# A graph convolution on one core: the preparation in front of the edge loop is cut to the first 512 tiles, and the rest is spread over the first pass

## The chip, the core and the metric

The kernel runs on one core of a Trainium2 chip. The metric is the device time of one execution in microseconds (us). TensorE is called PE, VectorE DVE, ScalarE ACT, GpSimd POOL and SyncE SP; DMAs are issued from the queues of SP, ACT and POOL (SPq, ACTq, POOLq in the profile) and run on 16 DMA engines that all queues share.

## The reference

There are N = 12500 nodes with 128 features and E = 400000 edges with 20 attributes and a weight each. The targets `dst` are sorted.

```python
h = jnp.maximum(_layernorm(x, axis=-1), 0.0)
h = h @ W_in2f.T                                     # N x 128
Wij = smu(edge_attr @ W_f1.T + b_f1) @ W_f2.T + b_f2   # E x 128, smu is a smooth GELU-like bend
Wij = Wij * edge_weight[:, None]
x_ij = h[dst] * Wij                                  # gather by dst, which is sorted
agg = segment_sum(x_ij, src, num_segments=N)         # scatter by src, which is random
out = x + smu(agg @ W_o1.T + b_o1) @ W_o2.T + b_o2
```

So for each edge a row of `h` is read at the edge's target, multiplied by a filter that two small layers compute from the attributes, and summed into the row of its source.

## The kernel before

**Tiles.** 128 edges are a tile; there are NT = 3125 tiles. Four tiles are a group (NG = 782), eight tiles a "super" (391), and the supers are split into seven passes (`PARTS`, six of 59 supers = 118 groups, and a last one of 37). Nodes are in NB = 98 bins of 128.

**Gather.** Since `dst` is sorted, the targets of a super lie within a window of 128 rows of `h`. `load(s)` on SP brings the attributes of super s (`f`), its targets relative to the first one (`rbc`, from the DRAM tensor `rel_dram`), reads the first target from `base_i` into a register and loads 128 rows of `h` from there (`hw`, from the DRAM tensor `h_dram`; three bf16 parts of each row). `pick` makes a one-hot matrix of `rbc` on DVE, and `gather` multiplies by it on PE. `hide`, `bend`, `smooth` and `weigh` are the two layers of the filter, `take` and `mix` the product, `turn` four PE transposes.

**Scatter.** `send` scales the rows by the edge weights on ACT and issues four indirect DMAs per group on POOL (line 562), one for each tile: each edge's row goes to a slot in the part of `buf<k>` (DRAM) that belongs to its source's bin. `bins`, `count`, `read` and `number` compute the slots from `hi_b` (the source's bin) with PE and DVE. While pass k+1 runs, `parts` reads back the slots of pass k (`fetch`), and sums each bin by a one-hot matmul (`choose`, `add`) into `agg`. After the last pass, the last slots are summed and the output layers run.

**Order.** PE, DVE, ACT and SP run in the order in which the code is written (`tc.manual_schedule`). In loop iteration g the engines turn and send group g, mix group g+1, hide and count group g+2 and make bins of group g+3, so DVE, ACT and PE run ahead of POOL by as much as the six buffers `ms` allow. An engine works strictly in order: what stands behind a waiting instruction waits too. This holds for the queues of SP and ACT as well, in which the DMA issues stand among the other instructions. A further wait is set by the framework: DMAs from SP and ACT share eight completion counters in turn, and a DMA waits until the DMA eight issues before it, on the same counter, has landed.

**In front of the loop (lines 216 to 313).** All of `dst` and `src` is loaded (ACT's queue, lines 221 and 228), all of `w_sb`, the first HEAD = 8 bins of x on SP (line 223), and the rest of x in four DMAs on POOL (lines 226 and 227). x is held in the memory of `agg` (`x_sb`). Then the relative targets of all tiles are computed (`rel`: a PE broadcast of the first targets, line 256; a DVE subtraction, line 259), transposed on PE (line 266), cast on ACT (line 267) and written to `rel_dram` on SP (line 268); their limits are reduced (lines 276 and 277); `hi_b` and `lo_b` are cut from `src` (lines 289 to 293); the statistics of the layer norm (`stats`), and the rows of `h` (`rows_of_h`, six steps for four bins: `normed` on DVE, `turned` on PE, `cut` on ACT, `product` on PE, `first_part` and `other_parts` on ACT and DVE, then a DMA into `h_dram`) are made for the first eight bins; two weights and a bias are folded.

**In the first pass.** `others` yields the remaining steps, and `step()` is called three times in each group: first the statistics of the 90 other bins, two at a time followed by two empty steps (141 calls, 47 groups), then one for the deviations, then six for each four bins of `h` (138 calls, 46 groups). The first pass reads only rows of `h` below HEAD * 128 (`base_i` is held to that by line 284, and `bad` records if it didn't suffice; a slow fallback at the end, which is not entered here, serves that case).

**Clearing.** Before slots are scattered into `buf<k>`, their tail is cleared from a zero tile on SP: 48 DMAs of 387 KB for the first pass within its first 38 groups, while the scatter already runs, and those of pass k+1 during pass k.

Of the kernel before, what the change touches and what calls it, by code (L numbers as in the profile page):

```python
# [9 lines left out]
F32 = mybir.dt.float32  # L10
BF = mybir.dt.bfloat16
I32 = mybir.dt.int32
F16 = mybir.dt.float16
AF = mybir.ActivationFunctionType
ALU = mybir.AluOpType
# [24 lines left out]
def gnn_kernel(  # L40
# [85 lines left out]
    nc.vector.memset(onesb, 1.0)  # L126
    bad = const.tile([P, 4 + 2 * EPOCHS], F32, name="bad")
    nc.vector.memset(bad, 0.0)
# [39 lines left out]
    HEAD = 8  # L168
# [47 lines left out]
    with tc.tile_pool(name="prep", bufs=1) as prep, \  # L216
            tc.tile_pool(name="node", bufs=3) as node, \
            tc.tile_pool(name="nps", bufs=2, space=PSUM) as nps:
        dst_i = prep.tile([P, NT], I32, name="dst_i")
        src_i = prep.tile([P, NT], I32, name="src_i")  # L220
        nc.scalar.dma_start(dst_i, dst_col)
        nc.vector.memset(x_sb[:, NB - 1, :], 0.0)
        nc.sync.dma_start(x_sb[:, 0:HEAD, :], bin_rows(x, 0, HEAD))
        nc.sync.dma_start(w_in, w_in_t)
        for a, n in chunks(NB - 1 - HEAD, 30):
            nc.gpsimd.dma_start(x_sb[:, HEAD + a:HEAD + a + n, :], bin_rows(x, HEAD + a, n))
        nc.gpsimd.dma_start(x_sb[:LASTB, NB - 1, :], x[(NB - 1) * P:N, :])
        nc.scalar.dma_start(src_i, src_col)
        nc.scalar.dma_start(w_sb, w_col)
        nc.vector.memset(w_f1, 0.0)  # L230
        nc.scalar.dma_start(w_f1[0:R, :], w_f1_t)
        nc.scalar.dma_start(w_f1[R:R + 1, :], b_f1)
        nc.scalar.dma_start(w_f2, w_f2_t)
        nc.scalar.dma_start(w_o1, w_o1_t)
        nc.scalar.dma_start(w_o2, w_o2_t)
        nc.scalar.dma_start(b1, b_o1.rearrange("o p -> p o"))
        nc.scalar.dma_start(b2row, b_f2)
        nc.scalar.dma_start(b2, b_f2.rearrange("o p -> p o"))
        nc.scalar.dma_start(bo2, b_o2.to_broadcast([P, P]))

        nc.vector.memset(zero, 0.0)
        clear(0, len(cleans) - 1, nc.sync)
        zero_b = prep.tile([P, 3 * D], BF, name="zero_b")
        nc.vector.memset(zero_b, 0.0)
        nc.scalar.dma_start(h_dram[NB * P:N + WIN, :], zero_b[:N + WIN - NB * P, :])


        nc.vector.tensor_copy(base_i[:, :], dst_i[0:1, 0:NT:SUP])
        base_f = prep.tile([1, NS], F32, name="base_f")
        nc.vector.tensor_copy(base_f, base_i)  # L250
        rel = prep.tile([P, NT], F32, name="rel")
        nc.vector.tensor_copy(rel, dst_i)
        S = GRP * P // SUP
        for a, n in chunks(NS, S):
            pb = nps.tile([P, S, SUP], F32, name="pb")
            nc.tensor.matmul(pb[:, :n], ones1, base_f[:, a:a + n].unsqueeze(2).to_broadcast([1, n, SUP]),
                             start=True, stop=True)
            w = min(NT - a * SUP, n * SUP)
            nc.vector.tensor_sub(rel[:, a * SUP:a * SUP + w], rel[:, a * SUP:a * SUP + w],
                                 pb.rearrange("p s t -> p (s t)")[:, :w])  # L260
        for a, m in chunks(NT // P, GRP) + [(NT // P, 0)]:
            pd = nps.tile([P, GRP, P], F32, name="pd")
            rb = node.tile([P, GRP, P], BF, name="rb")
            if m:
                for j in range(m):
                    nc.tensor.transpose(pd[:, j, :], rel[:, (a + j) * P:(a + j + 1) * P], ident)
                nc.scalar.activation(rb[:, :m], pd[:, :m], AF.Copy)
                nc.sync.dma_start(rel_dram[0, a * P * P:(a + m) * P * P].rearrange("(c t e) -> t c e", t=P, e=P),
                                  rb[:, :m])
            elif NT % P:  # L270
                m = NT % P
                nc.tensor.transpose(pd[:m, 0, :], rel[:, a * P:NT], ident)
                nc.scalar.activation(rb[:m, 0], pd[:m, 0], AF.Copy)
                nc.sync.dma_start(rel_dram[0, a * P * P:].rearrange("(t e) -> t e", e=P), rb[:m, 0])
        lh = prep.tile([P, 2], F32, name="lh")
        nc.vector.tensor_reduce(lh[:, 0:1], rel, op=ALU.min, axis=AX.X)
        nc.vector.tensor_reduce(lh[:, 1:2], rel, op=ALU.max, axis=AX.X)
        nc.vector.tensor_scalar(bad[:, 0:1], lh[:, 0:1], 0.0, None, op0=ALU.is_lt)
        nc.vector.tensor_scalar(bad[:, 1:2], lh[:, 1:2], float(WIN - 1), None, op0=ALU.is_gt)
        most = prep.tile([1, 1], F32, name="most")  # L280
        early = eps_of[0][1] + 3
        nc.vector.tensor_reduce(most, base_f[:, :early], op=ALU.max, axis=AX.X)
        nc.vector.tensor_scalar(bad[0:1, 2:3], most, float(HEAD * P - WIN), None, op0=ALU.is_gt)
        nc.vector.tensor_scalar(base_i[:, :early], base_f[:, :early], float(HEAD * P - WIN), None, op0=ALU.min)


        for a, n in chunks(NT, 625):
            part = node.tile([P, 625], I32, name="part")
            nc.vector.tensor_scalar(part[:, :n], src_i[:, a:a + n], 7, None, op0=ALU.arith_shift_right)
            nc.vector.tensor_copy(hi_b[:, a:a + n], part[:, :n])  # L290
            part = node.tile([P, 625], I32, name="part")
            nc.vector.tensor_scalar(part[:, :n], src_i[:, a:a + n], P - 1, None, op0=ALU.bitwise_and)
            nc.vector.tensor_copy(lo_b[:, a:a + n], part[:, :n])


        for b in range(HEAD):
            stats(node, b)
        deviations(0, HEAD)
        for b, n in chunks(HEAD, GRP):
            four = [node.tile([P, GRP, P], F32, name=f"four{i}") for i in range(3)]  # L300
            for step in rows_of_h(b, n, *four, node.tile([P, GRP, 3, D], BF, name="hs"),
                                  lambda name: nps.tile([P, GRP, P], F32, name=name)):
                step()

        nc.vector.tensor_scalar(w_f2, w_f2, GC, None, op0=ALU.mult)
        nc.vector.tensor_scalar(w_o2, w_o2, GC, None, op0=ALU.mult)

        nc.vector.tensor_scalar(bz, b1, ZS, None, op0=ALU.mult)
        b1w = prep.tile([P, P], F32, name="b1w")
        nc.vector.tensor_scalar(b1w, onesb, b1, LIN, op0=ALU.mult, op1=ALU.mult)  # L310
        pb1 = nps.tile([P, GRP, P], F32, name="pd")[:, 0, :]
        nc.tensor.matmul(pb1, b1w, w_o2, start=True, stop=True)
        nc.vector.tensor_add(bo2, bo2, pb1)

# [28 lines left out]
    with tc.tile_pool(name="ld", bufs=4) as ld, \  # L343
# [9 lines left out]
        nc.vector.tensor_copy(irow_ps, irow)  # L353
        NF = 4
        fbufs = []
        for i in range(NF):
            fb = ld.tile([P, SUP * P], F32, name=f"f{i}", bufs=1)
            nc.vector.memset(fb, 1.0)
            fbufs.append(fb)
# [7 lines left out]
        def load(s):  # L367
            if s >= NS:
                return
            t0, nt = sups[s]  # L370
            e0, n = t0 * P, nt * P
            fb = fbufs[s % NF]
            nc.sync.dma_start(fb[0:R, :n], f_t[:, e0:e0 + n])
            rb = ld.tile([P, SUP * P], BF, name="rbc")
            nc.sync.dma_start(rb[:, :n], rel_dram[:, e0:e0 + n].to_broadcast([P, n]))
            hw = ld.tile([P, 3 * D], BF, name="hw")
            at = nc.sync.value_load(base_i[0:1, s:s + 1], min_val=0, max_val=N)
            nc.sync.dma_start(hw, h_dram[bass.ds(at, WIN), :])
            loaded[s] = (fb, rb, hw)
# [255 lines left out]
        for s in range(3):  # L635
            load(s)
        for s in range(2):
            pick(s)
        for g in range(3):
            bins(g)  # L640
        count(0)
        read(0)
        count(1)
        read(1)
        number(0)
# [5 lines left out]
        weigh(0)  # L651
        gather(0)
        take(0)
        mix(0)
        smooth(1)
        cleared = at_first = done = 0
        work = []

        hs = edge.tile([P, GRP, 3, D], BF, name="hs", bufs=1)

        def others():
            for b, n in chunks(NB - HEAD, 2):
                yield lambda b=b, n=n: [stats(edge, HEAD + b + j) for j in range(n)]
                yield None
                yield None
# [8 lines left out]
        def step():  # L674
            f = next(h_steps, None)
            if f:
                f()
# [227 lines left out]
```

## Time and profile before

| | |
|---|---|
| median of 3 runs | 4286.98 us (4285.12 to 4287.03) |
| profiled execution | 4295.33 us, of it span 4293.6 us |
| mean granted PE clock in it | 0.966 |
| busy in the span | PE 87%, DVE 74%, POOL 71%, ACT 66% |
| indirect DMAs on POOL | 3125, mean 967 ns |
| first indirect DMA starts at | 93.53 us |

The profiled execution is 8.35 us longer than the median of the runs. A page's row names a line, an engine, an operation and its tiles, then the count, the busy time and the mean of one in ns, and the idle time of the engine before it with what ended it. In a timeline a row starts with the start and the duration in us, and ends with the idle time before it in brackets.

### The profile page before, as it was taken

The numbers are of one execution on the slowest core, as the hardware profiler recorded it, in microseconds if no ns is written. First come the engines' busy times: TensorE is split into PE (matmuls) and PEld (weight loads), VectorE is DVE, ScalarE is ACT, GpSimd is POOL, SyncE is SP. The second block draws the span as 40 slices with busy tenths as digits, with TensorE's granted clock in tenths as the row PEclk, the third lists the DMA queues.
The fourth block names the chain that finished last, engine by engine and source line by source line (L and its number), as shares of the span: only waits on it lengthen the run. The fifth ranks groups of instructions, "written<-read, shape, count | busy, mean of one in ns | idle before, by whom it ended". The sixth has DMA issues, their size and how long they took to land.

```text
span 4293.6 us, 74022 instructions
## 1 busy us (share of the span) xinstructions
PE 3745.7 (87%) x18332; PEld 2305.2 (54%) x18596; DVE 3177.7 (74%) x8458; ACT 2825.2 (66%) x11054; POOL 3029.8 (71%) x3137
## 2 busy tenths in 40 slices
PE   4877786999997999979999979999889999799977
PEld 2334443655554655545655546555556555466666
DVE  5876675877776877768877768777678777688856
ACT  2777786776766777657766667767667767566610
POOL 1777677777777777777777777777777777777710
PEclk9999998999999999989999999999999999899989
DMA  6955565766665766647666657666576666466666
GB/s 186 218 144 165 162 185 150 204 208 197 196 180 182 211 207 195 202 148 209 208 201 196 197 164 213 195 198 202 146 205 197 188 183 187 145 204 197 192 192 179
DMA packets 457334, 808.89 MB, mean 188 GB/s; under 512 B 82228, under 2 KB 258630, under 8 KB 456512
## 3 DMA queue, kind: packets, MB, share of 16 engines
q1 hardware_dynamic: 328136, 573.65, 47.4%
q0 software_dynamic: 101504, 212.48, 15.5%
q10 hardware_dynamic: 27256, 17.94, 1.4%
q8 instruction: 150, 2.46, 0.3%
q14 instruction: 288, 2.36, 0.2%
HBM read 449.68 MB, written 354.07 MB: 187 GB/s over the span
## 4 chain that ended last, share of the span: by engine, by line
PE 33%; DMA 15%; DVE 13%; ACT 5%; issue 3%; POOL 1%; ACTq 0%; DVEq 0%; POOLq 0%; SPq 0%
DMA buf<-ms,ix 13%; PE pw L529 8%; PE pg L607 8%; PE pu L479 6%; PE ph L510 5%; PE pt L549 4%; DVE se L594 4%; DVE mt L539 2%; DMA hg<-in_x 2%; ACT ms L559 2%; DVE sm L495 1%; ACT ge L487 1%; ACT jk L457 1%; DVE co L414 1%; DVE agg L620 1%
## 5 line engine op out<-in xcount | busy, mean ns | idle before, releaser
L562 POOL DMA_INDIRECT buf<-ms,ix x3125 | 3023.1, 967 | 1065.4 <-issue 278.4
L559 ACT ACTIVATE ms<-pt,w_sb 128x128 f32<-128x128 f32 x3125 | 905.0, 390 | 501.9 <-DMA buf<-ms,ix 287.0
L607 PEld LDWEIGHTS pg<-se,rw 128*128 128x128 f32 x7840 | 1075.3, 193 | 168.2 <-issue 23.4
L607 PE MATMUL pg<-se,rw 128*128 128x128 f32 x7840 | 1098.7, 276 | 19.7 <-DVE se L594 19.7
L457 ACT ACTIVATE jk<-pc,nbig 128x98 f32<-128x98 f32 x3125 | 1029.3, 354 | 12.9 <-PE pc L428 12.5
L529 PE MATMUL pw<-sm,w_f 128*128 128x512 f32 x1564 | 897.5, 656 | 27.1 <-DVE sm L495 19.6
L539 DVE SCALAR_TENSOR_TENSOR mt<-pw,b,hg 128x512 f32<-128x512 f32 x782 | 583.8, 747 | 416.7 <-ACT hg L518 414.2
L479 PE MATMUL pu<-f,w_f 128*128 128x512 f32 x1564 | 808.1, 599 | 2.6 <-DVE sm L495 2.5
L549 PE MATMUL pt<-ident,mt 128*128 128x128 f32 x3125 | 497.6, 282 | 347.3 <-DVE mt L539 343.8
L487 ACT ACTIVATE ge<-pu 128x512 f32<-128x512 f32 x782 | 469.4, 600 | 471.9 <-PE pu L479 459.9
L594 DVE TENSOR_TENSOR se<-irow_ps,rw 128x1536 f32<-128x1536 f32 x327 | 571.8, 1749 | 162.0 <-DMA rw<-buf 135.8
L457 ACT ACTIVATION_READ_ACCUMULATOR jk<-pc,nbig 128x1 f32 x3125 | 682.9, 219 | 0.0
L495 DVE SCALAR_TENSOR_TENSOR sm<-pu,ge 128x512 f32<-128x512 f32 x782 | 536.1, 686 | 186.0 <-ACT ge L487 175.2
L510 PE MATMUL ph<-oh,hw 128*128 128x512 bf16 (+1 forms) x2082 | 635.2, 387 | 15.5 <-issue 2.0
L518 ACT ACTIVATE hg<-ph 128x512 f32<-128x512 f32 x782 | 469.4, 600 | 228.8 <-PE ph L510 226.8
L549 PEld LDWEIGHTS pt<-ident,mt 128*128 128x128 f32 x3125 | 352.5, 142 | 439.3 <-DVE mt L539 434.5
L414 DVE TENSOR_TENSOR co<-co,po 128x98 f16<-128x98 f16 x2351 | 502.3, 214 | 81.2
L510 PEld LDWEIGHTS <-hw 128*128 128x128 bf16 x2346 | 234.2, 100 | 560.6 <-issue 460.0
L400 DVE TENSOR_TENSOR po<-irow_ps,hi_b 128x392 f16<-128x392 f32 x782 | 433.9, 555 | 0.0
L529 PEld LDWEIGHTS pw<-sm,w_f 128*128 128x128 f32 x1564 | 237.7, 191 | 170.7 <-DVE sm L495 167.1
L427 PE MATMUL pc<-co,ones_h 128*128 128x392 f16 x782 | 257.7, 330 | 14.0 <-DVE co L414 14.0
L479 PEld LDWEIGHTS pu<-f,w_f 128*128 128x128 f32 x1564 | 250.4, 194 | 23.6 <-DVE sm L495 4.1
(114 smaller groups left out, 1675.2 us busy)
## 6 DMA issues: line engine op xcount, KB each, us to landing
rw<-buf SPq DMA_DIRECT2D x326, 774.0 KB
buf<-zero SPq DMA_DIRECT2D x294, 387.0 KB
rbc<-rel_dram SPq DMA_DIRECT2D x390, 256.0 KB
buf<-ms,ix POOLq DMA_INDIRECT x3125
hw<-h_dram SPq DMA_DIRECT2D x391, 96.0 KB
f<-in_f_t SPq DMA_DIRECT2D x390, 80.0 KB
buf<-zero SPq DMA_DIRECT2D x49, 258.0 KB
h_dram<-hs SPq DMA_DIRECT2D x24, 384.0 KB
```

Of the source, the lines that this page charges most:

```text
L414: nc.vector.tensor_add(co[:, j], co[:, j - 1], po[:, j - 1])
L457: nc.scalar.activation(jk, pc[:, j], AF.Relu, bias=nbig, accum_out=sl[:, j:j + 1])
L479: nc.tensor.matmul(pu[:, :n], w_f1, loaded[g // PER][0][:, o:o + n], start=True, stop=True)
L495: nc.vector.scalar_tensor_tensor(sm[:, :n], units_of.pop(g)[:, :n], LIN, hidden[g][:, :n], op0=ALU.mult, op1=ALU.add)
L510: nc.tensor.matmul(ph[:, :n], hw[:, q * D:(q + 1) * D], oh[:, o:o + n], start=(q == 0), stop=(q == 2))
L529: nc.tensor.matmul(pw[:, :n], w_f2, hidden.pop(g)[:, :n], start=True, stop=True)
L539: nc.vector.scalar_tensor_tensor(mt[:, :n], pws.pop(g)[:, :n], b2, rows_of.pop(g)[:, :n], op0=ALU.add, op1=ALU.mult)
L549: nc.tensor.transpose(pt[:, j, :], mt[:, j * P:(j + 1) * P], ident)
L559: nc.scalar.activation(ms[:, j, 0:P], pt[:, j], AF.Copy, scale=w_sb[:, t + j:t + j + 1])
L562: i = nc.gpsimd.indirect_dma_start(out=bufs[k][:, :], out_offset=bass.IndirectOffsetOnAxis(ap=ix[:, j:j + 1], axis=0), in_=ms[:, j, :], in ...
L594: nc.vector.tensor_tensor(se[:, :m], irow_ps.unsqueeze(1).to_broadcast([P, m, P]), rows_in[c][:, :m, P:P + 1].to_broadcast([P, m, P]), op= ...
L607: nc.tensor.matmul(pgs[0][:, g, :], rows_in[c][:, o, 0:P], sel[c][:, o, :], start=(q == 0), stop=(q == Q[k] - 1))
```

## The change

The pools and the code in front of the loop go. What the first pass needs of it (the relative targets, bins and places of the first CH = 512 tiles, that is 64 supers, and the rows of `h` of HEAD = 4 bins) is made within the loop's own pools, in an order written out by hand together with the loop's first steps. The same for the other six chunks of 512 tiles becomes nine steps each (`head_of`), one bin's statistics after each; then the other statistics, the deviations, six steps for each four bins of `h`, and the folding of the output bias: COUNT = 276 steps. `step()` spreads them evenly over 318 calls (106 of the 118 groups). The bulk of x moves from POOL's queue to ACT's, in three DMAs of 31 bins and one of 84 rows, behind the small loads; `w_sb` comes in two parts. The check of the limits is reduced at the end.

```diff
-    HEAD = 8
+    HEAD = 4
...
-        nc.scalar.dma_start(dst_i, dst_col)
-        nc.sync.dma_start(x_sb[:, 0:HEAD, :], bin_rows(x, 0, HEAD))
-        for a, n in chunks(NB - 1 - HEAD, 30):
-            nc.gpsimd.dma_start(x_sb[:, HEAD + a:HEAD + a + n, :], bin_rows(x, HEAD + a, n))
-        nc.scalar.dma_start(src_i, src_col)
-        nc.scalar.dma_start(w_sb, w_col)
...
-        nc.vector.tensor_copy(rel, dst_i)
-        for a, n in chunks(NS, S):
...
-        for a, m in chunks(NT // P, GRP) + [(NT // P, 0)]:
...
-        for b in range(HEAD):
-            stats(node, b)
-        deviations(0, HEAD)
-        for b, n in chunks(HEAD, GRP):
...
+        def head_of(c):
+            a, n = c * CH, min(CH, NT - c * CH)
+            s0, m = a // SUP, (n + SUP - 1) // SUP
+            rw = rowp.tile([P, ROWS, ROW], F32, name="rw").rearrange("p q r -> p (q r)")
+            di, si, rel = rw[:, 0:n].bitcast(I32), rw[:, CH:CH + n].bitcast(I32), rw[:, 2 * CH:2 * CH + n]
+            if c:
+                rb = hs[:, :, 0, :]
...
+            def fetched():
+                nc.sync.dma_start(di, dst_col[:, a:a + n])
+                nc.sync.dma_start(si, src_col[:, a:a + n])
+            def based():
+                nc.vector.tensor_copy(base_i[:, s0:s0 + m], di[0:1, 0:n:SUP])
+                nc.vector.tensor_copy(base_f[:, :m], base_i[:, s0:s0 + m])
+                nc.vector.tensor_copy(rel, di)
+            def spread():
...
+                nc.tensor.matmul(flat, ones1, base_f[:, :m].unsqueeze(2).to_broadcast([1, m, SUP]),
+                                 start=True, stop=True)
+            def lowered():
+                nc.vector.tensor_sub(rel, rel, kept[0].rearrange("p j e -> p (j e)")[:, :n])
+            def turned():
...
+                    nc.tensor.transpose(pd[:w, j, :], rel[:, o:o + w], ident)
+            def written():
...
+                    nc.scalar.activation(rb[:, :whole], kept[0][:, :whole], AF.Copy)
+                    nc.sync.dma_start(rel_dram[0, a * P:(a + whole * P) * P].rearrange("(c t e) -> t c e", t=P, e=P),
+                                      rb[:, :whole])
...
+            def limits():
+                nc.vector.tensor_reduce(lh[:, 0, c:c + 1], rel, op=ALU.min, axis=AX.X)
+                nc.vector.tensor_reduce(lh[:, 1, c:c + 1], rel, op=ALU.max, axis=AX.X)
+            def bounded():
...
+            def binned():
+                nc.vector.tensor_scalar(di, si, 7, None, op0=ALU.arith_shift_right)
+                nc.vector.tensor_copy(hi_b[:, a:a + n], di)
+            def placed():
+                nc.vector.tensor_scalar(di, si, P - 1, None, op0=ALU.bitwise_and)
+                nc.vector.tensor_copy(lo_b[:, a:a + n], di)
...
+        one = head_of(0)
+        one["fetched"]()
+        nc.scalar.dma_start(x_sb[:, 0:HEAD, :], bin_rows(x, 0, HEAD))
+        nc.scalar.dma_start(w_in, w_in_t)
...
+        nc.scalar.dma_start(w_sb[:, 0:CH], w_col[:, 0:CH])
+        for i in range(NF):
+            fill(i)
+        nc.vector.memset(zero, 0.0)
+        clear(0, len(cleans) - 1, nc.scalar)
+        nc.vector.memset(x_sb[:, NB - 1, :], 0.0)
+        for a, n in chunks(NB - 1 - HEAD, 31):
+            nc.scalar.dma_start(x_sb[:, HEAD + a:HEAD + a + n, :], bin_rows(x, HEAD + a, n))
+        nc.scalar.dma_start(x_sb[:LASTB, NB - 1, :], x[(NB - 1) * P:N, :])
+        nc.scalar.dma_start(w_sb[:, CH:NT], w_col[:, CH:NT])
+        nc.scalar.dma_start(w_o1, w_o1_t)
+        nc.scalar.dma_start(w_o2, w_o2_t)
+        nc.scalar.dma_start(b1, b_o1.rearrange("o p -> p o"))
+        nc.scalar.dma_start(b2row, b_f2)
+        nc.scalar.dma_start(bo2, b_o2.to_broadcast([P, P]))
...
         for s in range(3):
+            nc.sync.dma_start(fbufs[s][0:R, :], f_t[:, s * SUP * P:(s + 1) * SUP * P])
+        one["based"]()
+        one["spread"]()
+        one["bounded"]()
+        one["lowered"]()
+        one["turned"]()
+        one["written"]()
+        nc.vector.tensor_scalar(w_f2, w_f2, GC, None, op0=ALU.mult)
+        for b in range(HEAD):
+            stats(edge, b)
+        deviations(0, HEAD)
+        rw = rowp.tile([P, ROWS, ROW], F32, name="rw")
+        for step in rows_of_h(0, HEAD, *[rw[:, j * GRP:(j + 1) * GRP, 0:P] for j in range(3)], hs, bank):
+            step()
+        for s in range(3):
             load(s)
-        for s in range(2):
-            pick(s)
-        for g in range(3):
-            bins(g)
-        count(0)
-        read(0)
-        count(1)
-        read(1)
-        number(0)
+        one["binned"]()
+        bins(0)
         hide(0)
         bend(0)
         smooth(0)
         hide(1)
         bend(1)
         weigh(0)
+        count(0)
+        read(0)
+        one["placed"]()
+        pick(0)
         gather(0)
+        number(0)
         take(0)
         mix(0)
         smooth(1)
+        bins(1)
+        count(1)
+        read(1)
+        pick(1)
+        bins(2)
...
         def others():
-            for b, n in chunks(NB - HEAD, 2):
-                yield lambda b=b, n=n: [stats(edge, HEAD + b + j) for j in range(n)]
-                yield None
-                yield None
+            yield one["limits"]
+            yield zeroed
+            left = list(range(HEAD, NB))
+            for c in range(1, NC):
+                it = head_of(c)
+                for name in ("fetched", "based", "spread", "lowered", "turned", "written", "binned", "placed", "limits"):
+                    yield it[name]
+                    if left:
+                        yield lambda b=left.pop(0): stats(edge, b)
+            while left:
+                two, left = left[:2], left[2:]
+                yield lambda two=two: [stats(edge, b) for b in two]
             yield lambda: deviations(HEAD, NB)
...
+            yield output_bias
+
+        COUNT = 2 + 18 * (NC - 1) + (NB - HEAD - 9 * (NC - 1) + 1) // 2 + 1 + 6 * -(-(NB - HEAD) // GRP) + 1
...
         def step():
-            f = next(h_steps, None)
-            if f:
-                f()
+            nonlocal taken_steps, slot
+            slot += 1
+            while taken_steps < COUNT and taken_steps * 3 * (eps_of[0][1] * PER - 12) < slot * COUNT:
+                next(h_steps)()
+                taken_steps += 1
...
+        nc.vector.tensor_reduce(ends[:, 0:1], lh[:, 0], op=ALU.min, axis=AX.X)
+        nc.vector.tensor_reduce(ends[:, 1:2], lh[:, 1], op=ALU.max, axis=AX.X)
+        nc.vector.tensor_scalar(bad[:, 0:1], ends[:, 0:1], 0.0, None, op0=ALU.is_lt)
+        nc.vector.tensor_scalar(bad[:, 1:2], ends[:, 1:2], float(WIN - 1), None, op0=ALU.is_gt)
```

## The prediction

> **What bounds the kernel now.** I read the page first, then POOL's timeline at the start, in the plain part and in the h part of the first pass, then the mixing instruction (line 539, once per group) as a clock of the other engines, then the timeline of the first 100 us with the SP and ACT queues.
>
> ```profile
> PE 3745.7 (87%) x18332; PEld 2305.2 (54%) x18596; DVE 3177.7 (74%) x8458; ACT 2825.2 (66%) x11054; POOL 3029.8 (71%) x3137
> L562 POOL DMA_INDIRECT buf<-ms,ix x3125 | 3023.1, 967 | 1065.4 <-issue 278.4
> ...
> 93.53 1.04 POOL L562 DMA_INDIRECT buf<-ms,ix  x1 [86.25 <-DVE ix L466]
> ...
> 602.11 0.96 POOL L562 DMA_INDIRECT buf<-ms,ix  x1 [0.30 <-ACT ge L487]
> 603.38 0.96 POOL L562 DMA_INDIRECT buf<-ms,ix  x1 [0.30 <-ACT jk L457]
> ...
> 474.95 1.39 POOL L562 DMA_INDIRECT buf<-ms,ix  x1 [2.38 <-ACT hs L208]
> ```
>
> PE is busiest on the page (87%), but POOL sets the pace: two scatters start 1.265 us apart whatever the idle time is put down to (0.96 busy, 0.30 between), so a group of four costs 5.06 us, and 3125 of them 3953 us of the 4293.6. Idle POOL time beyond the 0.30 is in two places: 93.53 us before the first scatter, and an h part around 420 to 575 us.
>
> ```profile
> L539 DVE SCALAR_TENSOR_TENSOR mt<-pw,b,hg x5: 745/746/750, 462.9 to 486.9; 128x512 f32<-128x512 f32 x5
> ...
> L539 DVE SCALAR_TENSOR_TENSOR mt<-pw,b,hg x5: 743/746/751, 123.6 to 139.8; 128x512 f32<-128x512 f32 x5
> ...
> 597.00:645.00 48.00, 36.68 (x38) 1.00 0.70 194
> 440.00:488.00 48.00, 32.34 (x32) 0.93 0.52 155
> ...
> PE pg L193 <- DVE rw L187: 21.1, 12, 1.8
> ```
>
> Four groups of the other engines take 16.2 us beside the statistics (4.05 each), also without any step (597 to 613), but 24.0 us (6.0 each) with three h steps a group. At 4.05 they run ahead of POOL: from mixing a group to its first scatter is 2.3 us at group 0 and saturates at about 26.5 us (six `ms` buffers); when they bound, it is 4.9. The lead of 21.6 us is eaten from group 47 on; from group 64 POOL gets 32 scatters where the plain part gets 38. By its start times in the trace, groups 64 to 89 take 156.7 us instead of 26 x 5.06 = 131.6: 25 us lost. At the end of the pass the engines wait for POOL (DVE sits 20.6 us for the first read-back), so a lead left there is worth nothing.
>
> ```profile
> 8.06 0.36 ACTq L233 DMA_DIRECT2D w_f<-in_w_f_t  x1
> 30.36 0.36 ACTq L234 DMA_DIRECT2D w_o<-in_w_o_t  x1
> 30.36 0.49 DVE L176 BATCH_NORM_STATS2 st<-agg 128x6 f32<-128x128 f32 x2 [27.71 <-DMA agg<-in_x]
> ...
> 70.50 0.50 SPq L375 DMA_DIRECT2D rbc<-rel_dram  x1
> 72.39 0.37 SPq L378 DMA_DIRECT2D hw<-h_dram  x1
> ```
>
> The 93.5 us are 30 of loading, 40 of preparing all tiles, 23 from the first `rbc` to the first scatter. And ACT's queue stood 22 us before line 234: its completion counter was that of x's first eight bins, which landed at 30.36 (the statistics start then too). That matters below.
>
> **The change, part by part.**
>
> *The start.* A first guess is "only 1 MB to load": wrong, because bulk x now stands in ACT's own queue, and the compiled order with its waits shows who waits: ACT's last load (`bo2`) for the second x chunk, the first `rel_dram` write on SP for the third, the first `rbc` load for the rest of `w_sb`. ACT's first activation stands behind `bo2`. So:
> - DVE's memsets: preface 1.3, four small ones about 1.0, four `f` at 1.07, `zero` 0.70: 7.6 us. Then ACT clears the last bin and issues x at about 8; first packets 2 us later, as in the trace (issue 0.75, first packet 2.05).
> - x is 11,988 rows of 512 B. Such packets on ACT's queue take 28 ns in the output stage: / 16 engines, 7 us a chunk. Chunk two lands at about 25, three at 32, the rest of `w_sb` (1.34 MB at the 350 GB/s of the first 20 us) at 36.
> - ACT free at 25.4, table load 1.28, cast 0.60. Then the h chain: table 1.28, `rstd` 0.30, and from the reciprocal to the `h_dram` issue 8.4 in before for eight bins (59.86 to 68.22), I take 7.5 for four: 36.4. `rel_dram` lands about then.
> - `rbc` issued at 36.8, landed 3.4 later (as the first one in before) at 40.2; `hw` issued 3.4 after the last `h_dram` issue (69.0 to 72.39 in before): 39.8, landed 42.
> - DVE behind the h rows: bins and slots 0.8 + 1.5, `smooth` 0.69: 39.5. In before `smooth(0)` to the first scatter is 7.35 us (86.18 to 93.53). The hand-made order puts `count(0)`, `count(1)`, `bins(1)`, and `read(1)` ahead of group 0's transposes and rows: 1.0 + 0.8 on PE, 1.5 on DVE, about 1.3 on ACT: 12 in all.
>
> First scatter at about 52: **-41.5 us**. Ends: 47 (DMA faster, PE out of its slow start, where a 512-column pass took 0.9 us and not 0.5) and 62 (ACT held until all of x and `w_sb` landed).
>
> *The removed preparation* of chunks 1 to 6 (two reductions of 3.4, casts, 24 transposes) is in that difference. It comes back in the pass. Per chunk by DVE rows: 512/3125 of the 3.4 reductions twice 0.6, subtraction 0.69, cast 0.34, base 0.26, four bin instructions at 0.40: 4.1; PE two broadcast passes 1.0 and four transposes 1.1; ACT 0.6; three DMAs on SP. Together 6.8 us of engine time. Four bins of h are 6.6 us (DVE 1.1 + 0.69 + 0.69, PE 1.1 + 1.15, ACT 0.60 + 0.62 + 0.63) and cost 2 x (6.03 - 4.05) = 4.0 us of the engines' common pace. So I take 4.5 per chunk, plus waits: `based` makes DVE wait for `dst` two or three calls after its fetch, 3 to 7 us; a 256 KB load among the clears lands 5 to 7 us after issue (`rbc` in the trace from 100 to 165 us). Queued behind it are `smooth` and `bins`, then PE and ACT. One long and two short waits, 5 us in all, go into the pace; the first chunk comes with no lead, **+2 us**. (SP's later loads are three supers ahead.)
>
> Here a rule speaks against the change. The Trainium skill's "DMA: Bandwidth & Descriptors", section "Anatomy of one DMA", gives about 2.0 us fixed plus bytes/436 GB/s for a transfer: 2.6 us for each 256 KB piece by estimate, 31 us for the twelve, if they were waited for in turn. The trace's busy pass has 5 to 7 us each instead, more than the rule; but waited for is only what the two calls between do not cover. I use the trace.
>
> *Lead.* Chunks: 41 groups at 4.05 + (6 x 4.5 + 5)/41 = 4.83, below 5.06: lead +9, from 2.3 to about 10. Then 20 calls of statistics, 7.7 groups at 4.05: +8, so 18, that is 13 above the bound state's 4.9.
>
> *The h part.* 24 x 6 = 144 steps at 276/318 per call are 55 groups at 4.05 + 2.60 x 0.66 = 5.77: deficit 39 us, less 13 of lead: 26 lost. Before 25: **+1**. (Full lead: 18 lost. No lead: 39. Bound below: if the cover grew with thinner steps, 0.) The last 12 groups rebuild 12 us, more than the boundary needs (about 10).
>
> *Casts beside POOL.* The skill's "SBUF — State Buffer", section "Who interferes with whom", says that copy, cast and tensor_scalar on DVE can take the port pair shared with GpSimd and block it outright. While the cuts ran before the loop, POOL was idle; now 30 stand beside scatters. A full block of 0.4 each would be 12 us. In the trace the 42 scatters that overlap a `normed` instruction last 1.095 us against 0.965, those beside `pick` 0.993 against 0.963. By those rows 30 x 0.03 to 0.13, 1 to 4 us: **+1**.
>
> *The rest.* POOL loses four DMA issues (6.7 us, before its long wait: 0). Four small DVE reductions at the end stand among idle DVE time of 1 to 2 us per step: 0, at worst +0.7. The `h_dram` padding, `w_o2` and `bo2` folds (1.2 us DVE) go into the lead. HEAD 4 holds the early reads below row 384; no cost.
>
> Sum: -41.5 + 2 + 1 + 1 = -37.5. Against the profiled 4295.33 that is 4258; the median of the runs is 8.35 lower, so 4249.
>
> **The rivals.**
> - *Start less early*: ACT's loads hold everything (first scatter at 62), or the chunks eat the lead (13 us more lost in the h part). Gain 15 to 28: 4259 to 4272. For it: the 22 us that ACTq stood in before. Against: only chunk two is waited for.
> - *The h part gets cheaper*: thinner steps fall beside POOL's pace; 18 to 0 lost, gain 45 to 63: 4224 to 4242. For: 5.77 is only 0.7 above 5.06. Against: in-order waits (PE on line 187) do not shrink with spacing.
> - *Slower*: DVE waits at `based` for each chunk's targets, behind the clears. Place: the first 41 groups. With the h part at 39 (no lead), +14, and the start's -41.5, the pass becomes slower once the chunks' part loses over 27.5 us to POOL, a pace of 5.73, 11.5 us a chunk and not 5.3. With 14 a chunk, 6.1: 43 lost, +15: 4302. For: DMA share 0.99 there. Against: that is six waits of nearly 9 us each.
> - *Nothing* (4287): the change does not do what it says, since the first `rbc` still waits for nearly the whole load. For: it does, by the order. Against: the load would have to last 40 us longer to cost what is saved, and in before all of it, and more, had landed by 38.
>
> **How the numbers follow.** Forecast 0.50 (4240 to 4258), less early 0.22, cheaper h part 0.19, slower 0.06, nothing 0.03. Range 4226 to 4268: the two side cases but their far ends. Runs of before differ by 0.05%; about 0.2% (8.6 us) is what a measurement can tell. Faster 0.90, same 0.04, slower 0.06.
>
> **What would show it.** First scatter at 47 to 62 us, ACT's first activation right after the `bo2` issue, at about 25; the mixing row 4.6 to 5.0 us apart in groups 1 to 41 and about 5.8 in groups 50 to 106; POOL gapless to about group 70, then 15 to 30 us lost; from group 118 on the trace as before, 35 to 45 us earlier. Wrong if the first scatter is later than 65, or POOL shows gaps at `based` in the first 40 groups.

## The result and the profile after

| | before | changed |
|---|---|---|
| median of the runs | 4286.05 us (4283.49 to 4287.03) | 4252.33 us (4248.00 to 4254.09) |
| profiled execution, span in it | 4295.33, 4293.6 us | 4248.00, 4245.9 us |
| first scatter starts at | 93.53 us | 57.42 us |
| POOL's loss in groups 0 to 118 | 28.7 us | 22.5 us |

The ratio is 0.9921, with a 95% interval of 0.9904 to 0.9938: 34 us faster. A later series of five rounds gave 4254.66 against 4289.92 us, 0.9914 (0.9901 to 0.9928): 35 us. In six of the experiments' runs (e4 to e9) every kernel took some 23% longer, the kernel before too (5293 to 5300 us), and those runs are compared only with that.

"POOL's loss" is used throughout: the time from the first scatter of one group to that of a later one, less 5.06 us for each group between. It comes from the start times in the trace. The first pass is groups 0 to 118. Its h part, the steps that make the rows of `h`, begins at group 50 in the changed kernel. In the kernel before it begins at group 45 and not 47: its statistics take 45 pairs of three calls, 135 calls and not 141.

The profile of the changed kernel (scatter now line 572, mix line 549, `normed` line 191), two rows of the page:

```profile
PE 3726.3 (88%) x18332; PEld 2294.6 (54%) x18596; DVE 3179.1 (75%) x8498; ACT 2818.5 (66%) x11057; POOL 3013.6 (71%) x3133
L572 POOL DMA_INDIRECT buf<-ms,ix x3125 | 3012.7, 964 | 1032.7 <-issue 257.3
```

POOL does the same 3125 scatters. Its idle time before them falls from 1065.4 to 1032.7 us, which is most of what these two profiles differ by; the scatters themselves take 10.4 us less (967 and 964 ns each). DVE and ACT are as busy as before to within 7 us, PE to within 20. The start, from the timeline (start and duration in us, then the queue or engine; in brackets the idle time before it), and one row of the waits of SP's queue up to 60 us:

```profile
7.43 0.34 ACTq L163 DMA_DIRECT2D buf<-zero  x1
...
8.00 0.83 ACTq L360 DMA_DIRECT2D agg<-in_x  x1
...
9.29 5.71 ACTq L360 DMA_DIRECT2D agg<-in_x  x1
...
15.46 6.46 ACTq L360 DMA_DIRECT2D agg<-in_x  x1
22.01 6.84 ACTq L361 DMA_DIRECT2D agg<-in_x  x1
28.89 0.38 ACTq L362 DMA_DIRECT2D w_sb<-in_w_col  x1
...
31.09 0.33 ACTq L367 DMA_DIRECT2D bo<-in_b_o  x1
31.46 1.28 ACT L314 ACT_TABLE_LOAD   x1 [16.03 <-DMA b2row<-in_b_f]
32.75 0.60 ACT L314 ACTIVATE oh<-pg 128x512 bf16<-128x512 f32 x1
...
33.38 0.41 SPq L315 DMA_DIRECT2D rel_dram<-oh  x1
42.39 0.41 SPq L214 DMA_DIRECT2D h_dram<-hs  x1
42.89 0.45 SPq L385 DMA_DIRECT2D rbc<-rel_dram  x1
45.17 0.38 SPq L388 DMA_DIRECT2D hw<-h_dram  x1
...
57.42 1.11 POOL L572 DMA_INDIRECT buf<-ms,ix  x1 [55.85 <-DVE lh L324]
...
SPq L315 <- DMA agg<-in_x: 26.3, 1, 26.3
```

Read the second column of ACT's queue. Issuing a DMA takes 0.2 to 0.9 us, and so does the first large piece of x (31 bins, 3968 rows: 0.83). But each of the three issues behind such a piece lasts 5.71, 6.46 and 6.84 us, the last of them for 84 rows only. No wait on a semaphore is shown there. A piece of 2.03 MB takes 7 us at the 290 GB/s that the DMA part of the trace has from 13 to 30 us, so by these rows the queue takes about one piece ahead, and the next issue lasts until there is room. SP's write to `rel_dram` waited 26.3 us for the third piece, until about 33.0, and then 0.4 for ACT's cast, so that write could not have gone much earlier with ACT free sooner; what came late through ACT is the h chain, `h_dram` at 42.39. ACT's first activation is at 32.75 us, and from ACT free (31.46) to the first scatter it is 26.0 us.

The pace of the other engines in the chunks' part and in the h part (line 549, once a group: count, first and last start), the windows answer for the h part (after the times: PE, PEld, DVE, ACT, POOL busy with instruction counts, granted clock, DMA share, GB/s), and the one row for `based` in the waits from 57 to 310 us:

```profile
L549 DVE SCALAR_TENSOR_TENSOR mt<-pw,b,hg x26: 732/748/752, 143.0 to 259.7; 128x512 f32<-128x512 f32 x26
...
L549 DVE SCALAR_TENSOR_TENSOR mt<-pw,b,hg x21: 737/749/752, 451.5 to 564.2; 128x512 f32<-128x512 f32 x21
...
450.00:570.00 120.00, 95.85 (x381) 48.54 (x386) 84.77 (x258) 87.71 (x326) 86.25 (x88) 0.96 0.61 170
...
DVE base_i L292 <- DMA rw<-in_dst_col: 1.9, 2, 1.4
```

26 groups in 116.7 us are 4.67 apart while chunks are prepared, so the engines stay ahead of POOL. In the h part 21 groups in 112.7 us are 5.64 apart, against 6.0 before, and POOL gets 88 instructions in 120 us, where the kernel before got 32 in 48 and an unhindered POOL 95 in 120.

### The profile page after: what moved, and what is told of

It is laid out like the page before. It is cut to its first block, busy times and chain, and to the rows that moved or that the text cites. A ratio compares the mean times of both kernels' runs of the same rounds, so it can differ in the third digit from the quotient of the medians.

```text
span 4245.9 us, 74047 instructions
## 1 busy us (share of the span) xinstructions
PE 3726.3 (88%) x18332; PEld 2294.6 (54%) x18596; DVE 3179.1 (75%) x8498; ACT 2818.5 (66%) x11057; POOL 3013.6 (71%) x3133
## 4 chain that ended last, share of the span: by engine, by line
PE 45%; DMA 21%; DVE 19%; ACT 9%; issue 4%; ACTq 1%; POOL 1%; DVEq 0%; SPq 0%; POOLq 0%
DMA buf<-ms,ix 17%; PE pw L539 12%; PE pg L617 10%; PE pu L489 8%; PE ph L520 7%; PE pt L559 5%; DVE se L604 5%; DVE mt L549 4%; ACT ms L569 3%; DVE sm L505 3%; ACT jk L467 2%; ACT ge L497 2%; DMA hg<-in_x 2%; DVE co L424 1%; DVE po L410 1%
## 5 line engine op out<-in xcount | busy, mean ns | idle before, releaser
L572 POOL DMA_INDIRECT buf<-ms,ix x3125 | 3012.7, 964 | 1032.7 <-issue 257.3
L617 PEld LDWEIGHTS pg<-se,rw 128*128 128x128 f32 x7840 | 1074.1, 193 | 171.3 <-issue 22.4
L539 PE MATMUL pw<-sm,w_f 128*128 128x512 f32 x1564 | 890.9, 652 | 37.9 <-DVE sm L505 32.7
```

Source lines behind the costliest of these rows:

```text
L539: nc.tensor.matmul(pw[:, :n], w_f2, hidden.pop(g)[:, :n], start=True, stop=True)
L572: i = nc.gpsimd.indirect_dma_start(out=bufs[k][:, :], out_offset=bass.IndirectOffsetOnAxis(ap=ix[:, j:j + 1], axis=0), in_=ms[:, j, :], in ...
L617: nc.tensor.matmul(pgs[0][:, g, :], rows_in[c][:, o, 0:P], sel[c][:, o, :], start=(q == 0), stop=(q == Q[k] - 1))
```

## The experiments

All ratios are to the kernel before on the same chip. What the runs showed of POOL's loss (us):

The name of a row fits the kernel before and the changed one. With one step at each call (e1, e11) the h part is groups 44 to 92, in e2 27 to 106, in e10 31 to 110.

| groups | before | changed | e0 | e1 | e2 | e3 | e10 | e11 |
|---|---|---|---|---|---|---|---|---|
| 0 to 42 (chunks) | 2.2 | 5.1 | 6.9 | 4.5 | 2.6 | 8.3 | 33.2 | 4.1 |
| 42 to 64 | 0.5 | 1.1 | 1.0 | 16.9 | 1.4 | 2.0 | 1.4 | 2.7 |
| 64 to 107 (h) | 26.0 | 16.1 | 11.6 | 33.9 | 1.5 | 14.6 | 3.4 | 15.4 |
| 107 to 118 | 0 | 0.2 | 0.7 | 0 | 0 | 0.1 | -0.1 | 0.2 |
| first pass | 28.7 | 22.5 | 20.2 | 55.3 | 5.5 | 25.0 | 37.9 | 22.4 |
| first scatter at | 93.53 | 57.42 | 57.37 | 58.99 | 93.72 | 44.39 | 44.60 | 56.51 |

**e0: the changed kernel again.** No edit; a second profile and a tighter ratio for the series.

> The changed kernel once more, unchanged. The two profiled executions differ by 47 us, the medians by 34, so the size of the gain is not settled. Theory A (the gain is what the first pass shows: first scatter 36 us earlier, and about 6 us net in the rest of the pass): about 42 us below the kernel before, within 3. Rival (part of what the one profile shows is the scatter of single executions): 30 to 36 us below, and the profile of this run shows the same start and first pass but a different sum over the later passes.

4254.66 us, 0.9914 (0.9901 to 0.9928). The gain of 35 us lies where the rival had it (30 to 36), not theory A (42). The first pass repeats within 2.3 us and the start within 0.06 us. The later passes, whose code no kernel here changes, lose 14.3 us in the first profile of the changed kernel, 24.9 in this one and 20.9 in before's: single profiles differ by some 10 us there.

**e1: one step at each call, not evenly spread.**

```diff
-            while taken_steps < COUNT and taken_steps * 3 * (eps_of[0][1] * PER - 12) < slot * COUNT:
+            if taken_steps < COUNT:
```

> The changed kernel with the 276 steps taken one at each call (92 groups) instead of evenly over 318 calls (106 groups): undoes the even spreading alone. Theory A (each h step costs 0.66 us of the other engines' pace, and only the deficit against POOL's 5.06 us, less the lead, is lost): the h part takes 48 groups at 6.0, deficit 46, less a lead of 16 to 20, so 26 to 30 us lost there instead of 16; 10 to 14 us slower than the changed kernel, first scatter at the same time. Rival (an h chunk's in-order waits cost the same however wide the steps stand, so the sum lost is the same): within 3 us of the changed kernel.

4285.17 us, 0.9988 (0.9979 to 0.9997). 30.5 us slower than the changed kernel, where 10 to 14 were expected: POOL's loss in the first pass is 55.3 us against 22.5, and 28.7 in the kernel before, so that of the 34.5 us that its start gains over before 26.6 are given back. The steps are the same; only where they fall differs. The even spreading therefore carries the change's gain, as long as nothing else puts the steps in a good place (e11 below).

**e2: only the spreading.** The kernel before, with its 184 real steps spread over 318 calls and everything in front of the loop untouched.

```diff
                 yield lambda two=two: [stats(edge, b) for b in two]
-                yield None
-                yield None
...
+        COUNT = (NB - HEAD + 1) // 2 + 1 + 6 * -(-(NB - HEAD) // GRP)
...
-            f = next(h_steps, None)
-            if f:
-                f()
...
+            while taken_steps < COUNT and taken_steps * 3 * (eps_of[0][1] * PER - 12) < slot * COUNT:
+                next(h_steps)()
+                taken_steps += 1
```

> The kernel before, start untouched, with its 184 real steps (no empty ones) spread evenly over 318 calls: the other half of the change alone. Theory A: 1.74 steps a group, pace 5.2 in the h part of 79 groups, deficit 11 us, below the lead of 21: the 25 us lost in groups 64 to 92 go to nearly 0, so 20 to 25 us below the kernel before; first scatter at 93.5 as before. Rival (waits do not shrink with spacing): less than 8 us gained.

4270.43 us, 0.9956 (0.9942 to 0.9969): 19.5 us faster with the first scatter as late as before, just under theory A's 20 to 25. Its h part, in the windows of the trace:

```profile
450.00:570.00 120.00, 97.35 (x369) 47.99 (x377) 85.10 (x262) 89.74 (x342) 91.33 (x95) 0.94 0.59 166
```

POOL has 95 instructions in 120 us, its full pace: the h part's loss is gone (26.0 to 1.5 us). In the changed kernel the chunks' steps take calls of their own, so the h steps come closer together again, and 16.1 of it are back.

**e3: bulk x and the rest of `w_sb` on POOL's queue.**

```diff
-            nc.scalar.dma_start(x_sb[:, HEAD + a:HEAD + a + n, :], bin_rows(x, HEAD + a, n))
-        nc.scalar.dma_start(x_sb[:LASTB, NB - 1, :], x[(NB - 1) * P:N, :])
-        nc.scalar.dma_start(w_sb[:, CH:NT], w_col[:, CH:NT])
+            nc.gpsimd.dma_start(x_sb[:, HEAD + a:HEAD + a + n, :], bin_rows(x, HEAD + a, n))
+        nc.gpsimd.dma_start(x_sb[:LASTB, NB - 1, :], x[(NB - 1) * P:N, :])
+        nc.gpsimd.dma_start(w_sb[:, CH:NT], w_col[:, CH:NT])
```

> The changed kernel with bulk x and the rest of the weights issued on POOL's queue again instead of ACT's. Theory A (ACT stood until 31.5 us in its own queue because issuing three loads of 3968 rows took it 5.7, 6.5 and 6.8 us; the head waits for that, not for data of its own): ACT's first activation falls to about 13 us, the first scatter to 38 to 42, and 15 to 19 us are gained over the changed kernel. Rival (the DMA engines are full with x either way, and the head's small loads starve beside POOL's 4 KB packets as the first eight bins of x did in the kernel before, until 30 us): first scatter at 52 to 58, no gain.

4242.92 us, 0.9885 (0.9870 to 0.9900): 11.7 us below the changed kernel in the same series, and the lowest ratio seen. Theory A had 15 to 19 us and a first scatter at 38 to 42. Its start in the timeline:

```profile
1.58 5.47 POOL L360 DMA_DIRECT2D agg<-in_x  x3
...
44.39 1.02 POOL L572 DMA_INDIRECT buf<-ms,ix  x1 [35.39 <-DVE lh L324]
...
16.58 0.34 ACTq L367 DMA_DIRECT2D bo<-in_b_o  x1
16.95 1.28 ACT L314 ACT_TABLE_LOAD   x1 [16.95 <-DMA w_sb<-in_w_col]
...
18.87 0.41 SPq L315 DMA_DIRECT2D rel_dram<-oh  x1
...
33.07 0.34 SPq L385 DMA_DIRECT2D rbc<-rel_dram  x1
```

ACT is free at 16.95 instead of 31.46 us, so the issues behind the pieces of x were what held it. The price is on POOL's own engine while it has nothing else to do: 5.47 us. But the start moves by 13.0 and not by those 14.5 us, and two new waits stand in it. `bo2` on ACT waits until 16.58 for the first part of `w_sb`, which shares the DMA engines with x; and the write to `rel_dram`, issued at 18.87, moves its packets only between 23.8 and 32.3 us, so the first `rbc` is issued 14.2 us after it, 4.7 us of that in SP's wait for this landing (9.5 in the changed kernel, where the h rows set it). So the rival is right in part: small transfers do wait beside POOL's 4 KB packets. The first pass loses 2 to 5 us more. With 13.0 from the start, 8 to 11 remain, beside 11.7 measured.

**e4, e5: one per call, shifted by two calls or one.** The kernel of e1 with two empty steps (e5: one) ahead of the deviations. With two, `normed` falls on the second call after the mix, as it does in before; with none (e1) on the third.

```diff
+            for _ in range(2):
+                yield lambda: None
             yield lambda: deviations(HEAD, NB)
...
```

> One step at each call as in e1, with two empty steps ahead of the deviations, so that each h step falls on the same one of a group's three calls as in the kernel before (the norm in the second call, after the mix). In e1 the h part ran at 6.2 us a group and lost 49 us, where the kernel before ran at 6.0 with the same three steps a group. Theory A (which of the three calls a step falls on sets what it makes wait): the pace falls back to 6.0, some 8 to 10 us less lost than in e1. Rival (something else of the changed kernel slows the h part, so the alignment does nothing): 6.2 as in e1, within 3 us of it.

> The third alignment: e1 with one empty step ahead of the deviations (the norm in the first call, between sending and mixing). Theory A: a pace of its own, not that of e1; between 5.6 and 6.5 us a group, since the even spreading, which goes through all alignments, averages 5.66 at 2.6 steps, 0.62 a step, or 5.9 at three. Rival: 6.2 as in e1.

**e6: e3, and steps paced by an estimate of their cost.** Weights of 0.5 for a step of a chunk, 0.25 for a pair of statistics, 0.67 for an h step, over 336 calls.

```diff
...
-            while taken_steps < COUNT and taken_steps * 3 * (eps_of[0][1] * PER - 12) < slot * COUNT:
-                next(h_steps)()
-                taken_steps += 1
+            while spent * CALLS < slot * WHOLE:
+                w, f = next(h_steps, (WHOLE, None))
+                spent += w
+                if f:
+                    f()
...
```

> e3 (bulk x on POOL's queue), with the steps spread evenly by their cost and not by their number: chunk steps 0.5, a bin's statistics 0.05 or 0.25 for two, h steps 0.67, over 336 calls (112 groups). Theory A (what is lost in the pass is the work over POOL's pace; a lead that stands at its cap of 26 us from group 40 to 50 is work that could have been done there): the h part starts at about group 31 and runs at about 5.2 us a group, so 5 to 8 us lost in groups 50 to 118 instead of 16; 6 to 11 us below e3. Rival (what counts is the h chunks' waits and not where they stand): within 3 us of e3.

These three took 5265.82 (e4), 5256.23 (e5) and 5274.27 us (e6), against 5293.16 for before; 0.9947 (0.9917 to 0.9977), 0.9922 (0.9890 to 0.9953), 0.9973 (0.9943 to 1.0002). They do not decide. A plain stretch of e4, in the second pass:

```profile
1000.00:1120.00 120.00, 98.52 (x457) 59.79 (x454) 74.53 (x194) 66.79 (x266) 75.82 (x79) 0.91 0.52 161
```

and of the kernel before in its first profile:

```profile
1000.00:1120.00 120.00, 109.76 (x545) 67.74 (x552) 91.39 (x241) 84.69 (x340) 91.06 (x96) 1.00 0.67 197
```

POOL has 79 instructions against 96, at a granted PE clock of 0.91 against 1.00. Over the whole profiles only PE's instructions are longer in e4 (377 ns on the mean, 357 before); DVE's, ACT's and POOL's agree within 1%. So POOL waits in plain groups too, and what a step costs it cannot be seen. The same three kernels a second time (e7 is e6, e8 is e4, e9 is e5) met the same:

> The kernel of e6 again, since in e4 to e6 every kernel, that before too (5293 us), ran at 6.4 us a group and not at POOL's 5.06. Expected as for e6. Theory A: 5 to 8 us lost in groups 50 to 118 instead of 16, so 6 to 11 us below e3, about 0.9865 of the kernel before. Rival: within 3 us of e3, 0.9885.

> The kernel of e4 again, for the same reason, with the same expectations. Theory A: the h part at 6.0 us a group as in the kernel before, 8 to 10 us less lost than in e1, about 0.9965 of the kernel before. Rival: 6.2 as in e1, 0.9988.

> The kernel of e5 again, for the same reason. Theory A: a pace of its own, not that of e1, between 5.6 and 6.5 us a group. Rival: 6.2 as in e1.

5264.79 (e7), 5262.94 (e8) and 5254.81 us (e9) against 5299.51; 0.9932 (0.9899 to 0.9965), 0.9939 (0.9910 to 0.9967), 0.9895 (0.9855 to 0.9935). Inconclusive again; why these series ran at the lower clock is not known. The shift by one call has no other run; what it does where POOL sets the pace stays open.

**e10: e6 a third time.**

> The kernel of e6 once more. If the plain groups run at POOL's 5.06 us: Theory A: 5 to 8 us lost in groups 50 to 118 instead of the 15 to 16 of e3, so 6 to 11 us below e3, about 0.9865 of the kernel before. Rival: within 3 us of e3, 0.9885.

4248.21 us, 0.9915 (0.9902 to 0.9929): not below e3 but above it (0.9885). The h part does become nearly free (3.4), but by these weights the chunks' steps come denser, and groups 0 to 42 lose 33.2 us: their pace there is 5.9 and 5.7 us a group, above POOL's 5.06, at a time when there is little lead (5 to 8 us). PE's granted clock there is 0.88, against 0.97 in the changed kernel, so the pace is not set by the number of steps alone, and which ratio of the weights would be right is not shown. The loss has moved, not gone.

**e11: e4 a third time.**

> The kernel of e4 once more: h steps on the same calls of a group as in the kernel before. If the plain groups run at 5.06 us: Theory A: h part at 6.0 us a group, 8 to 10 us less lost than in e1, about 0.9965 of the kernel before. Rival: 6.2 as in e1, 0.9988.

4245.18 us, 0.9913 (0.9898 to 0.9928), against 0.9988 in e1. Two empty steps, 0.75% or 32 us. POOL's loss falls by 32.9 (55.3 to 22.4), as much as the time. This is far more than theory A had (0.9965): the mixing row comes every 5.6 us in groups 50 to 92, where the theory took the 6.0 of the kernel before, with its h steps on the same calls. The windows from 330 to 450 us, first of e1:

```profile
330.00:450.00 120.00, 94.93 (x365) 48.64 (x369) 78.51 (x237) 80.43 (x297) 73.70 (x76) 0.89 0.52 153
```

and of e11:

```profile
330.00:450.00 120.00, 96.95 (x403) 51.01 (x411) 89.01 (x267) 88.73 (x331) 90.24 (x92) 0.97 0.63 181
```

POOL does 76 instructions in the one and 92 in the other, and no engine is full in either, so the engines wait for each other. PE's granted clock differs too, 0.89 against 0.97; more on that below. The timeline of e1 shows how it hangs together, PE's rows of one group and then DVE's:

```profile
364.80 1.11 DVE L191 TENSOR_SCALAR rw<-agg,mv,rstd 128x128 f32<-128x128 f32 x4
...
365.20 1.10 PE L197 MATMUL pg<-ident,rw 128*128 128x128 f32 x4 [2.18 <-DVE rw L191]
366.13 1.02 PE L539 MATMUL pw<-sm,w_f 128*128 128x512 f32 x2
366.99 0.81 PE L520 MATMUL ph<-oh,hw 128*128 128x512 bf16 x3
...
368.47 0.75 DVE L549 SCALAR_TENSOR_TENSOR mt<-pw,b,hg 128x512 f32<-128x512 f32 x1 [2.41 <-ACT hg L528]
```

In e1 `normed` (line 191) is the last step of a group and stands at the end of DVE's work. PE's transposes of it (line 197) are the first step of the next group, ahead of `weigh` (539) and `gather` (520). So PE idles 2.18 us for DVE, and then DVE idles 2.41 us for `take` (528), which waits for that `gather`. The clock was granted in full here. The waits of the two kernels from 330 to 430 us (total us, times, longest), e1:

```profile
ACT hg L528 <- PE ph L520: 29.2, 8, 4.4
DVE mt L549 <- ACT hg L528: 26.1, 8, 4.0
...
PE pg L197 <- DVE rw L191: 17.5, 8, 2.2
```

and e11:

```profile
PE pg L197 <- DVE rw L191: 12.2, 9, 1.4
...
DVE mt L549 <- ACT hg L528: 6.8, 8, 1.8
...
ACT hg L528 <- PE ph L520: 2.6, 2, 1.4
```

PE still waits for `normed`, with 12.2 instead of 17.5 us, but the mix behind it hardly does: 26.1 becomes 6.8.

The waits are not all of it. The trace's clock records have stretches of 3.4 or 6.8 us at half clock: from the mix of group 45 to that of group 91 they add up to 57.7 us in e1, 17.1 in e11 and 41.0 in the kernel before. These 46 groups take 286.4, 259.8 and 276.9 us. If PE's work set the pace all the time, a stretch at half clock would cost half its length; by this estimate up to 20 of the 27 us between e1 and e11, and up to 12 of the 17 between before and e11, go with the clock. In groups 0 to 42, where e1 and e11 run the same steps on the same calls, both have 6.8 us at half clock, so the lower clock of e1 comes with the place of its steps. How the waits and the clock bring each other about is not shown.

Nor is the call all that places a step. A chunk of `h` takes two groups, and `load` and `pick` stand in even groups only. `normed` falls in odd groups in before (45) and in e1 (43), but in an even one in e11 (44), so there are six places and not three, and e11 differs from before by one group. What that does by itself has no run.

Since e11 is as fast as the changed kernel without any spreading, spreading in itself is not needed. A likely reading, not tested by itself, is that it lets the steps fall on all calls in turn, so that the bad place is met only now and then.

## Why the prediction was right, and where its steps were not

The time fell at the place and by the mechanism that it named: the first scatter comes earlier, and the first pass loses POOL no more than before. Several terms of the sum were off, and the two largest in opposite directions.

- **The start: -36.1 us, not -41.5.** The step that failed is "ACT free at 25.4". It took ACT's last load to wait for the second chunk of x, "landed at about 25", and took the issues themselves to cost nothing. The rows show 31.46: three issues of 5.71, 6.46 and 6.84 us, one behind each piece. The 62 us end of the prediction had "ACT held until all of x and `w_sb` landed": the place was right, but ACT was held by issuing, and only until the last piece of x was nearly through. e3, where nothing of this stands in ACT's queue, shows it. From ACT free to the first scatter it took 26.6 us (25.4 to 52); measured 26.0. That chain through `rel`, `h_dram`, `rbc` and the hand-made order stood. The named end, 47 to 62, holds 57.42.
- **The chunks' part: +2 became +3 (+4.7 in e0).** Pace 4.73 over groups 0 to 42 (4.83 predicted); loss 5.1 us, where the kernel before had 2.2. The waits at `based` were put at 5 us into the pace and are 1.9 us in all. So the twelve fetches are not waited for in turn: the rule of the Trainium skill's "DMA: Bandwidth & Descriptors", "Anatomy of one DMA", gave 31 us for that case, and the choice to count only what two calls do not cover was right. That section is about DMAs that GpSimd issues, and these fetches are issued by SP.
- **Casts beside POOL: +1 became less than 1.** The 25 scatters that overlap one of the changed code's cuts and casts (lines 294, 333, 334, 337, 338) last 0.978 us on the mean (0.954 to 1.082), the others 0.964; in e0 it is 22 with 0.995, two of them 1.21. A block in full at each, as the rule of the Trainium skill's "SBUF — State Buffer", "Who interferes with whom", allows, would have been 0.4 us each, and is not seen. Beside `normed` the mean is 1.014 us; of those 36 scatters 3 last 1.39 to 1.43, and in the kernel before 13 of 42 last 1.39 to 1.40, so single ones may be blocked.
- **The lead: 25.0 us at group 50, not 18.** The prediction's own terms add up to 2.3 + 9.4 + 7.8 = 19.5. It began at 5.7 us instead of 2.3, the pace was lower than estimated, and the losses in the chunks' part kept POOL back.
- **The h part: -10 us, not +1.** The pace was nearly right, 5.66 to 5.76 us against 5.77 (5.6 in e0, which lost 11.6 us). With the full lead the prediction's own figure was 18 us lost; the trace has 16.1. So the mis-sized term is the lead. The loss lies in the range of the rival "h part gets cheaper" (18 to 0), but not through that rival's reason, since the steps were hardly cheaper than forecast.
- **The rest at nothing:** from the last group's scatter to the end of the span it is 198.7 us before and 200.0 after (198.2 in e0), so the four reductions at the end do not show.

By the ledger the profiled executions differ by 36.1 at the start, 6.2 in the first pass, 6.6 in later passes and -1.3 after the last group: the 47.6 us between their spans. Between the medians there are 34. The two profiled executions lie 9.3 above and 4.3 below their medians, which makes up the difference. The 6.6 us of later passes are chance by e0, where they are -4.0. Start and first pass together, 42 to 45 us, are still some 8 to 9 us more than the medians show (their interval reaches to 41 or 42), and where a usual execution gives those back stays open. So the "-37.5" was near the result in part by luck: a start that was forecast 5 us too good met an h part forecast 10 us too bad, and the 42 us or more that the terms really come to are not all found in the medians.

Why the spread steps cost 5.7 a group and not 6.0 was put down to fewer steps in each group. e1 against e11 shows that their number is not all of it: with one step in each call in both, groups 42 to 107 lose 50.8 or 18.1 us by where `normed` falls. The prediction named the wait (PE on line 187) as the argument against its "cheaper" rival; it did not see that the wait's size depends on the place, nor that PE's granted clock falls with it (0.90 in e1 and 0.97 in e11, groups 45 to 91).

## What to carry to other kernels

Where a trace shows it as here, count what is issued behind a DMA of thousands of rows as held for about that DMA's transfer time, with all that follows on that engine, and put such DMAs on an engine with nothing to do (here POOL before its first scatter, 11.7 us). When steps are woven into an in-order loop, look for the pair "producer at the end of one engine's group, consumer at the front of another's": the same steps two calls later were worth 32 us here, and the count of the work is the same. Look at the granted clock of the two stretches before putting all of such a difference down to waits. An earlier start of the bound engine is only kept if the pace behind it is below its own: e1 started 35 us earlier than before, and ended 5 us earlier.

## What the hardware did that was not expected

- Behind a DMA of 3968 rows of 512 bytes the next issue on ACT's queue lasted 5.71 to 6.84 us, even one of 84 rows; the load of 512 rows and the issues after it took 0.23 to 0.9 us. The three large pieces issued by POOL took 5.47 us together.
- Beside such bulk traffic small transfers wait long: in e3 a write of 128 KB to `rel_dram` moved its last packet 13.4 us after its issue; in the changed kernel, with x landed, 3.3 us.
- PE's granted clock fell to half for stretches of 3.4 or 6.8 us in the h part, for 57.7 us in e1 and 17.1 in e11 (groups 45 to 91), though the two kernels differ only in where the same steps stand.
